# A graph-attention layer on one core: scatters of a second sort held between gathers, and record loads moved from the GpSimd queue to the Sync queue

## The chip, the cores and the metric

The kernel runs on one core of one Trainium2 chip. Its time is device time in microseconds (us). The kernel before took 1815.98 us, the median of three runs (1813.75 to 1820.42). One further execution was taken with the hardware profiler and gives all durations below; in it "start" counts from the beginning of the span. TensorE is called PE in the profile (its weight loads PEld), VectorE DVE, ScalarE ACT, GpSimd POOL, and SyncE SP, which only issues transfers here.

## The reference

A layer of masked attention with 4096 targets, 4096 sources, a width of 512 and 8 heads of 64, followed by a feed-forward network and a last normalisation. All arithmetic is float32. The adjacency matrix is sparse: some 17 sources to a target. Cut to what matters:

```python
hs = layer_norm(x, ln1_scale, ln1_bias)              # sources
ht = layer_norm(h_target, ln1_scale, ln1_bias)       # targets
q = (ht @ Wq + bq).reshape(T, 8, 64) / sqrt(64)
k = (hs @ Wk + bk).reshape(S, 8, 64)
v = (hs @ Wv + bv).reshape(S, 8, 64)
logits = where(adj != 0, einsum('thd,shd->hts', q, k), -1e30)
ctx = einsum('hts,shd->thd', softmax(logits), v).reshape(T, 512)
ht = layer_norm(ht + ctx @ Wo + bo, ln2_scale, ln2_bias)
out = ht + gelu(ht @ W1) @ W2
return layer_norm(x + out)                           # no scale, no bias
```

## The kernel before

**Sparse attention by gathers.** The kernel does not compute all 4096 x 4096 logits. It finds the neighbours of every target as a list of row numbers, writes keys and values of all sources into a DRAM table `kvd` (one row of 1024 floats per source), and fetches, for a tile of 128 targets, neighbour number j of each target with one indirect transfer. A tile needs as many gathers as its longest list. So that tiles are even, the targets are sorted by degree: `CAPS_A` and `CAPS_B` (L374) give how many neighbours the sorted tiles may have.

**Two parts.** The 32 row blocks are handled in two halves of 16, part 0 and part 1 (`PARTS`). For each half, `edges(i)` (L717) builds lists from the adjacency rows, and `sort(part)` (L808) computes where each target goes in the sorted order and scatters its *record* (degree, target number, two normalisation numbers and up to 24 neighbours: 29 words) into the DRAM table `recs_d[part]`. The scatter of part 0 runs before attention begins; the lists and the sort of part 1 run beside the attention over the first half (the stream `other_lists`, L1444), and its 16 scatters (L854, in the profile `rec<-R,kv`) stand on the GpSimd queue among the gathers.

**What the attention does per tile.** `prefetch(i)` (L971) loads the records of sorted tile i from `recs_d` into one of six `rec` buffers (L980, in the profile `rec<-rec`); `front(i)` gathers the targets' rows (`tq<-in_L_gnn_h_target_dram`), normalises and projects them. `issue(k)` (L1059) gathers the keys and values of group k, three neighbours at a time (L1076, issued through `gather`, L966, so that the profile shows L967, `kv<-kvd,rec`), into a ring of 17 slots, 20 from the second half on. VectorE multiplies keys with queries (L1220), sums them to logits (L1225), ScalarE takes exponentials (L1229, L1238), VectorE scales values (L1184), and TensorE adds them up by transposing them into one PSUM tile (L1192). When L1192 of a group has read its slots they are free for later gathers: group k waits for L1192 of group k-5 or k-6. `finish` (L1078) divides, applies Wo (L1116), takes the second normalisation (statistics on VectorE L697, the power -1/2 on GpSimd L687, its use L692 and L1134) and transposes (L1143) for the feed-forward network.

**Long lists.** Two tiles, sorted tile 15 (39 neighbours) and tile 17 (38), have more than the 24 neighbours that a record holds. For them `rest_of` (L769) gathers the rest (`gid<-rest_d,rec`), and VectorE picks the next neighbours in two rounds of L779 and L780, and counts them (L783, L786).

**Feed-forward.** `feed(g)` (L1310) runs per pair of tiles: W1 (L1325), GELU on ScalarE (L1328), W2 (L1334). `end` normalises and scatters the result rows (L1302, `out_dram<-xt,tags`; the rows of x come by `xt<-in_x_dram,tags`).

**What sets the order.** The streams attention, feed-forward, lists of the second half and weights are woven in program order by costs (`_weave`, L400). A scheduler then fixes each engine's queue ahead of the run: it may move an instruction ahead of, or behind, others on its engine where its own estimate of times says so, unless an edge forbids it. [...] `tc.issue_after(ins)` adds such an edge: what is written inside the block stays behind `ins` on that engine's queue, without a semaphore. On GpSimd the queue before has, after the first half's gathers have run for some time, 9 scatters in a row, three gathers, the power L687, 6 scatters, and a little later the last one. On the Sync queue all adjacency loads (L714) and all stores of list rests (L767) come before anything that the change puts there; after it stands only the read of the final flag (L1453).

Of the kernel before, what the change touches and what calls it, by code (L numbers as in the profile page):

```python
# [1 line left out]

# [15 lines left out]
P = 128  # L18
# [360 lines left out]
RW = E0 + RE  # L379
# [64 lines left out]
def adj_resnorm_kernel(  # L444
# [33 lines left out]
    nc = tc.nc  # L478
# [34 lines left out]
    recs_d = [dram.tile([n * P, RW], I32, name=f"rec{i}") for i, (_, n) in enumerate(PARTS)]  # L513
# [19 lines left out]
    with tc.tile_pool(name="keep", bufs=1) as keep:  # L533
# [17 lines left out]
        with ExitStack() as late:  # L551
# [22 lines left out]
            def turn_of(name, places):  # L574
                turns[name] += 1
                return places[turns[name] % len(places)]
# [132 lines left out]
            def quarter(i, h):  # L709
# [4 lines left out]
                nc.sync.dma_start(a, adj[i * P:(i + 1) * P, h * QW:(h + 1) * QW])  # L714
                return a

            def edges(i):  # L717

                part = 1 if i >= NA else 0
                rec = Rs[part][:, i - PARTS[part][0], :]  # L720
                cand = lp.tile([P, SEG, 8], U16, name="cand", bufs=2)
                for h in range(NQ):
                    n = i * NQ + h
                    while len(adjs) < min(n + 2, NT * NQ):
                        adjs.append(quarter(*divmod(len(adjs), NQ)))
                    a, adjs[n] = adjs[n], None

                    sg = turn_of("signs", signs)
                    nc.scalar.activation(sg, a, AF.Sign, accum_out=dpart[:, i, h:h + 1])  # L729
                    ahead = min(n + DEEP - 1, n + 3 + n // 2)  # L730
                    while len(adjs) < min(max(n + 3, min(ahead, RINGED * NQ)), NT * NQ):
                        adjs.append(quarter(*divmod(len(adjs), NQ)))
                    wd = sg.bitcast(U16)
                    nc.vector.tensor_tensor(wd, wd, lio, ALU.mult)
                    for s, (w0, w1) in enumerate(SEGS):
                        nc.vector.max(cand[:, h * SQ + s, :], wd[:, w0:w1])  # L736
                    if h == 1:
                        keep_rest()
                    if h % 2 and moms:
                        moments(moms.pop(0))  # L740
                    yield 2.0
                dec = dec_w
                nc.vector.tensor_single_scalar(dec[:, 0], cand, 255, op=ALU.bitwise_and)
                nc.vector.tensor_single_scalar(dec[:, 1], cand, 8, op=ALU.logical_shift_right)
                gid = lp.tile([P, 2 * SEG, 8], F32, name="gid")
                dec = dec.rearrange("p b s e -> p (b s) e")
                off = segoff.rearrange("p b q s -> p (b q s)")
                nc.vector.scalar_tensor_tensor(gid, dec, 0.0,
                                               off.unsqueeze(2).to_broadcast([P, 2 * SEG, 8]),
                                               op0=ALU.is_gt, op1=ALU.mult)  # L750
                nc.vector.tensor_add(gid, gid, dec)
                flat = gid.rearrange("p s e -> p (s e)")
                for r in range(RE // 8):
                    top = rec[:, E0 + r * 8:E0 + (r + 1) * 8]
                    nc.vector.max(top, flat)  # L755
                    if r + 1 < RE // 8:
                        nc.vector.match_replace(flat, top, flat, 0.0)
                held.append((rest_d[i * P:(i + 1) * P, :], flat))
                has = lp.tile([P, MAXE], F32, name="ehas")
                nc.vector.tensor_scalar(has[:, :RE], rec[:, E0:E0 + RE], 0.0, 0.0, op0=ALU.is_gt,  # L760
                                        op1=ALU.add, accum_out=cnt[:, i:i + 1])
                yield 4.0

            def keep_rest():

                while held:
                    nc.sync.dma_start(*held.pop())  # L767
# [40 lines left out]
            def sort(part):  # L808

                i0, n = PARTS[part]  # L810
                me = slice(i0, i0 + n)
                pool, R = lp, Rs[part]
                nc.vector.tensor_reduce(deg[:, me], dpart[:, me, :], AX.X, ALU.add)
                nc.vector.tensor_copy(R[:, :, DEG], deg[:, me])
                dif, rank = tools[:, 928:928 + n], tools[:, 944:944 + n]
                ranki, b16 = tools[:, 960:960 + n].bitcast(I32), tools[:, 976:984].bitcast(BF16)
                nc.vector.scalar_tensor_tensor(dif, deg[:, me], float(RE), cnt[:, me], op0=ALU.min,
                                               op1=ALU.not_equal)
                nc.vector.tensor_reduce(bad[:, 1 + part:2 + part], dif, AX.X, ALU.max)
                nc.vector.tensor_scalar(dif, deg[:, me], 0.0, float(NB - 1), op0=ALU.max,  # L820
                                        op1=ALU.min)
                nc.vector.tensor_scalar(b16, dif, -1.0, float(NB - 1), op0=ALU.mult, op1=ALU.add)
                if part:
                    oh = turn_of("wide", wide).bitcast(BF16)
                else:
                    oh = wp.tile([P, NB * n], BF16, name="oh")
                oh = oh[:, :NB * n].rearrange("p (b i) -> p b i", b=NB)
                nc.vector.tensor_tensor(oh, b16.unsqueeze(1).to_broadcast([P, NB, n]),
                                        bins.unsqueeze(2).to_broadcast([P, NB, n]), ALU.is_equal)
                ohf = oh.rearrange("p b i -> p (b i)")  # L830
                pos = turn_of("wide", wide).bitcast(F32)
                pos = pos[:, :NB * n].rearrange("p (b i) -> p b i", b=NB)
                posf = pos.rearrange("p b i -> p (b i)")
                w = NB * n // 2
                yield 6.0
                for c in range(2):
                    sl = slice(c * w, (c + 1) * w)
                    pt = ps.tile([P, w], F32, name="t", bufs=2)
                    nc.tensor.matmul(pt, ones_bf, ohf[:, sl], start=True, stop=True)
                    nc.vector.tensor_tensor_scan(posf[:, sl], one_c.to_broadcast([P, w]), pt,  # L840
                                                 0.0 if c == 0 else posf[:, c * w - 1:c * w],
                                                 op0=ALU.mult, op1=ALU.add)
                yield 4.0
                for c in range(2):
                    sl = slice(c * w, (c + 1) * w)
                    pa = ps.tile([P, w], F32, name="t" if part else "cps", bufs=2)
                    nc.tensor.matmul(pa, lower, ohf[:, sl], start=True, stop=True)
                    nc.vector.tensor_add(posf[:, sl], pa, posf[:, sl])
                nc.vector.tensor_mul(pos, pos, oh)
                nc.vector.tensor_reduce(rank, pos.rearrange("p b i -> p i b"), AX.X, ALU.add)  # L850
                nc.vector.tensor_copy(ranki, rank)
                yield 10.0
                for i in range(n):
                    ins = nc.gpsimd.indirect_dma_start(  # L854
                        out=recs_d[part][:, :],
                        out_offset=bass.IndirectOffsetOnAxis(ap=ranki[:, i:i + 1], axis=0),
                        in_=R[:, i, :], in_offset=None)

                    tc.declare_no_dep(ins.ins, group=f"scatter{part}", reason="other rows")
                    tc.add_to_no_dep_group(f"scatter{part}", ins.ins)  # L860
                    yield 3.0 if part else 1.3
                done.add(part)
# [98 lines left out]
                        yield cost  # L961


            recs, tqs, h2Ts, done, ready, latest, newest = {}, {}, {}, set(), [], [], []

            def gather(dst, table, idx):  # L966
                nc.gpsimd.indirect_dma_start(  # L967
                    out=dst, out_offset=None, in_=table[:, :],
                    in_offset=bass.IndirectOffsetOnAxis(ap=idx, axis=0))

            def prefetch(i):  # L971
                if i >= NT or i in recs:
                    return
                r0 = TILES[i][0]
                part = 1 if r0 >= PARTS[1][0] * P else 0
                assert part in done
                r0 -= PARTS[part][0] * P
                rec = sp.tile([P, E0 + MAXE], I32, name="rec", bufs=6)

                nc.gpsimd.dma_start(rec[:, :RW], recs_d[part][r0:r0 + P, :])  # L980
                recs[i] = rec

            def front(i, idle=0):
# [503 lines left out]
```

## Time and profile before

| | |
|---|---|
| median of three runs | 1815.98 us (1813.75 to 1820.42) |
| the profiled execution | 1817.49 us |
| its span, first to last instruction | 1815.5 us |
| mean TensorE clock granted, share of full speed | 0.967 |
| TensorE busy | 1677.8 us, 92% |
| VectorE busy | 1436.5 us, 79% |
| ScalarE busy | 1224.1 us, 67% |
| GpSimd busy | 982.2 us, 54% |
| HBM traffic | 430.75 MB read, 30.89 MB written, 254 GB/s over the span |

The span starts with projections and lists of the first half; attention proper begins at about 300 us, the scatters of the second sort run from 627 to 665 us, the last gather starts at about 1663 us, and the rest is feed-forward work. "Busy" counts the time in which an instruction executes. [...] An engine idle in front of an instruction is shown with the instruction that released it ("<-"); "<-issue" means that the profile shows nothing it waited for. A busy share is an average over stages, so the question is always which wait ends last in the stage at hand.

### The profile page before, as it was taken

What the parts mean: (1) busy time and instruction counts of PE and PEld (TensorE: products, weight loads), DVE (VectorE), ACT (ScalarE), POOL (GpSimd) and SP (SyncE); (2) the same over time, 40 slices, a digit from 0 to 9 for tenths busy, and PEclk for the clock granted to TensorE, in tenths of its full rate; (3) what the DMA queues carried; (4) which work ended last, traced back from release to release, by engine and by line L of the source; (5) the groups of instructions that cost most, each with busy time, mean ns of one, the idle gap of its engine ahead of it and who ended that gap; (6) DMA issues with size and microseconds to landing.
All of it is one profiled execution on the core that took longest, in us unless ns stands there. A gap on an engine that the chain in (4) does not pass through costs nothing. (4 is left out here: it accounts for less than half of the span.)

```text
span 1815.5 us, 22973 instructions
## 1 busy us (share of the span) xinstructions
PE 1677.8 (92%) x7030; PEld 1097.9 (60%) x7030; DVE 1436.5 (79%) x2660; ACT 1224.1 (67%) x3121; POOL 982.2 (54%) x834
## 2 busy tenths in 40 slices
PE   7989984597999979999999989999999999999997
PEld 3434442465766656766776757666666666666664
DVE  6989876899999837777978989978878797988200
ACT  5767654487987736766778868877777676787311
POOL 1000144656566676766678788867575665763101
PEclk9999996698999989999999999999999999999998
DMA  9999968989887557777878878787776776774000
GB/s 344 366 380 372 344 198 319 404 287 332 271 305 256 201 173 243 258 255 267 273 263 302 293 260 295 249 285 250 241 266 222 248 251 238 244 248 153 18 6 26
DMA packets 140269, 463.26 MB, mean 255 GB/s; under 512 B 16500, under 2 KB 21672, under 8 KB 140136
## 3 DMA queue, kind: packets, MB, share of 16 engines
q0 software_dynamic: 96656, 342.64, 55.8%
q1 hardware_dynamic: 35664, 95.98, 15.0%
q10 hardware_dynamic: 7816, 23.08, 3.3%
q8 instruction: 58, 0.95, 0.2%
q14 instruction: 75, 0.61, 0.1%
HBM read 430.75 MB, written 30.89 MB: 254 GB/s over the span
## 5 line engine op out<-in xcount | busy, mean ns | idle before, releaser
L967 POOL DMA_INDIRECT kv<-kvd,rec x603 | 758.1, 1257 | 347.5 <-PE cps L1192 139.7
L1334 PE MATMUL po<-w,gt 128*128 128x512 f32 x1024 | 466.4, 598 | 16.2 <-ACT gt L1328 16.2
L1325 PE MATMUL pf<-h2T,w 128*128 128x256 f32 (+1 forms) x2176 | 465.9, 368 | 0.1
L1325 PEld LDWEIGHTS pf<-h2T,w 128*128 128x128 f32 x2176 | 389.3, 191 | 64.5 <-issue 20.3
L1220 DVE TENSOR_TENSOR kv<-kv,tq 128x1536 f32<-128x1536 f32 (+2 forms) x211 | 351.6, 1675 | 68.3 <-DMA kv<-kvd,rec 56.2
L1204 ACT ACTIVATE kv<-kv,pa 128x64 f32<-128x64 f32 x1520 | 391.0, 336 | 4.3
L1225 DVE TENSOR_REDUCE lg<-kv 128x24 f32<-128x1536 f32 (+2 forms) x211 | 350.1, 1666 | 1.4
L1334 PEld LDWEIGHTS po<-w,gt 128*128 128x128 f32 x1024 | 188.8, 192 | 212.4 <-issue 194.3
L1192 PEld LDWEIGHTS cps<-ident,kv 128*128 128x128 f32 x2008 | 240.2, 145 | 109.4 <-issue 59.2
L1192 PE MATMUL cps<-ident,kv 128*128 128x128 f32 x2008 | 264.5, 280 | 44.1 <-DVE kv L1184 24.5
L1184 DVE TENSOR_TENSOR kv<-kv,p 128x1024 f32<-128x1024 f32 (+1 forms) x211 | 251.0, 1193 | 22.8 <-ACT p L1229 20.3
L687 POOL TENSOR_TENSOR n_rs<-n_ve,mhalf 128x2 f32<-128x2 f32 (+2 forms) x51 | 50.8, 997 | 329.1 <-DVE n_ve L680 165.3
L729 ACT ACTIVATE kv<-kv 128x1024 uint8<-128x1024 int32 x128 | 134.9, 1056 | 100.0 <-DMA kv<-in_adj_dram 51.7
L1328 ACT ACTIVATE gt<-pf 128x512 f32<-128x512 f32 x128 | 76.4, 597 | 93.8 <-PE pf L1325 75.8
L1328 ACT ACT_TABLE_LOAD x104 | 133.4, 1283 | 1.7
L736 DVE MAX8 cand<-kv 128x8 uint16<-128x103 uint16 (+1 forms) x640 | 131.8, 252 | 0.8 <-DVE R L755 0.2
L930 PE MATMUL pq<-wk,h2T 128*128 128x512 f32 x256 | 120.8, 616 | 12.1 <-ACT tq L932 7.2
L1012 PE MATMUL t<-wq,tq 128*128 128x512 f32 x256 | 118.2, 605 | 5.6 <-ACT tq L1006 5.6
L930 PE MATMUL pq<-wv,h2T 128*128 128x512 f32 x256 | 115.5, 594 | 6.4 <-ACT kv L729 3.0
L1229 ACT ACTIVATE p<-lg 128x24 f32<-128x24 f32 (+2 forms) x179 | 39.2, 219 | 113.0 <-DVE lg L1225 88.8
L1116 PE MATMUL t<-wo,rb 128*128 128x512 f32 x256 | 115.2, 592 | 0.0
L930 PEld LDWEIGHTS pq<-wk,h2T 128*128 128x128 f32 x256 | 48.9, 197 | 69.9 <-issue 55.2
(160 smaller groups left out, 1582.2 us busy)
## 6 DMA issues: line engine op xcount, KB each, us to landing
kv<-in_adj_dram SPq DMA_DIRECT2D x128, 512.0 KB
kvd<-tq ACTq DMA_DIRECT2D x24, 512.0 KB
kv<-kvd,rec POOLq DMA_INDIRECT x603
kv<-in_L_gnn_h_target_dram SPq DMA_DIRECT2D x32, 256.0 KB
kv<-in_x_dram SPq DMA_DIRECT2D x15, 512.0 KB
rest_d<-gid SPq DMA_DIRECT2D x32, 160.0 KB
w<-in_L_gnn_W_dram SPq DMA_DIRECT2D x4, 1024.0 KB
kvd<-kv ACTq DMA_DIRECT2D x8, 512.0 KB
```

Source lines behind the costliest of these rows:

```text
L729: nc.scalar.activation(sg, a, AF.Sign, accum_out=dpart[:, i, h:h + 1])
L736: nc.vector.max(cand[:, h * SQ + s, :], wd[:, w0:w1])
L930: nc.tensor.matmul(pkv, hT[:, kc, j * P:(j + 1) * P], w[:, kc, :], start=kc == 0, stop=kc == KC - 1)
L967: nc.gpsimd.indirect_dma_start(out=dst, out_offset=None, in_=table[:, :], in_offset=bass.IndirectOffsetOnAxis(ap=idx, axis=0))
L1184: nc.vector.tensor_tensor(v4, v4, p[:, j0:j0 + m, :].unsqueeze(3) .to_broadcast([P, m, H, HD]), ALU.mult)
L1192: nc.tensor.matmul(cps[:, c, :], kv[:, j, D + c * P:D + (c + 1) * P], ident, is_transpose=True, start=j0 + j == 0 and c == 0, stop=j0 + n ...
L1204: newest[:] = [nc.scalar.mul(v, v, pa[:, hd:hd + 1]).ins]
L1220: nc.vector.tensor_tensor(kv[:, :n, :D], kv[:, :n, :D], tq[:, :D].unsqueeze(1).to_broadcast([P, n, D]), ALU.mult)
L1225: nc.vector.tensor_reduce(lg[:, :n, :], kv[:, :n, :D].rearrange("p j (h d) -> p j h d", h=H), AX.X, ALU.add)
L1325: nc.tensor.matmul(pf[:, k, :], w1[(f0 + k) // KC][:, kc, (f0 + k) % KC * P:((f0 + k) % KC + 1) * P], h2T[:, kc, :w], start=kc == 0, stop= ...
L1328: nc.scalar.activation(gt, pf, AF.Gelu_apprx_tanh)
L1334: nc.tensor.matmul(po[j], gt[:, k, j * P:(j + 1) * P], w2[(f0 + k) // KC][:, (f0 + k) % KC, :], start=False, stop=f0 + k == FC - 1, skip_g ...
```

## The change

Three edits. First, `gather` remembers the instruction that it issued, in the list `issues`. Second, each scatter of `sort` is written inside `behind(issues)`, which is `tc.issue_after` of the newest gather if there is one, and nothing otherwise; so part 0's scatters, before any gather, are as they were, and each scatter of part 1 stays behind the gather written last before it. Third, the record loads of part 1 (16 of 32) are issued from SP instead of GpSimd.

```diff
+            def behind(ins):
+                return tc.issue_after(ins[-1]) if ins else nullcontext()
...
                 for i in range(n):
-                    ins = nc.gpsimd.indirect_dma_start(
-                        out=recs_d[part][:, :],
-                        out_offset=bass.IndirectOffsetOnAxis(ap=ranki[:, i:i + 1], axis=0),
-                        in_=R[:, i, :], in_offset=None)
+                    with behind(issues):
+                        ins = nc.gpsimd.indirect_dma_start(
+                            out=recs_d[part][:, :],
+                            out_offset=bass.IndirectOffsetOnAxis(ap=ranki[:, i:i + 1], axis=0),
+                            in_=R[:, i, :], in_offset=None)
...
-            recs, tqs, h2Ts, done, ready, latest, newest = {}, {}, {}, set(), [], [], []
+            recs, tqs, h2Ts, done, ready, latest, newest, issues = {}, {}, {}, set(), [], [], [], []
 
             def gather(dst, table, idx):
-                nc.gpsimd.indirect_dma_start(
+                issues[:] = [nc.gpsimd.indirect_dma_start(
                     out=dst, out_offset=None, in_=table[:, :],
-                    in_offset=bass.IndirectOffsetOnAxis(ap=idx, axis=0))
+                    in_offset=bass.IndirectOffsetOnAxis(ap=idx, axis=0)).ins]
...
-                nc.gpsimd.dma_start(rec[:, :RW], recs_d[part][r0:r0 + P, :])
+                (nc.sync if part else nc.gpsimd).dma_start(rec[:, :RW], recs_d[part][r0:r0 + P, :])
```

The scheduler rearranges what is free to move. TensorE's queue comes out the same, instruction for instruction. On GpSimd, where the first scatter stood, the queue is now: 1 scatter, the record load of tile 14, 3 gathers, 2 scatters, the power L687, an output scatter, 3 gathers, 2 scatters, the row gathers and the second output scatter, and then groups of one to three gathers with one or two scatters after each; the last two scatters stand behind the gid gather of tile 15. On SP the 16 record loads follow each other behind the last store of list rests. ScalarE's queue has two more loads of its activation table and some neighbouring instructions exchanged; on VectorE some neighbours are exchanged, and the second round of L779 and L780 for tile 15 stands further back.

More of the change, by code (lines that the diff above doesn't have):

```diff
@@ L1 @@
-from contextlib import ExitStack
+from contextlib import ExitStack, nullcontext
 import concourse.bass as bass
```

## The prediction

> **What bounds the kernel now.** I read the page first, then the busy time by stretch of time, then what TensorE waited for, then the timelines of TensorE, VectorE and GpSimd around the scatters that the change moves. Page, part 1 (busy us, share of the span, instructions):
>
> ```profile
> PE 1677.8 (92%) x7030; PEld 1097.9 (60%) x7030; DVE 1436.5 (79%) x2660; ACT 1224.1 (67%) x3121; POOL 982.2 (54%) x834
> ```
>
> TensorE is idle for 1815.5 - 1677.8 = 138 us in all. Its instruction list is identical in both kernels, so the change can only alter how long it waits or at which clock it runs. In the groups of GpSimd instructions (count, busy us, mean ns, then idle time before them), the kinds at issue are these:
>
> ```profile
> L967 POOL DMA_INDIRECT kv<-kvd,rec x603 | 758.1, 1257 | 347.5 <-PE cps L1192 139.7 <-issue 121.0 <-DVE kv L1188 32.8
> L854 POOL DMA_INDIRECT rec<-R,kv x32 | 34.6, 1083 | 46.3 <-DVE cand L736 35.7 <-issue 8.7 <-DVE kv L851 1.5
> L980 POOL DMA_DIRECT2D rec<-rec x32 | 18.9, 593 | 22.3 <-DVE p L1083 8.9 <-DVE n_ve L680 5.3 <-DMA rec<-R,kv 4.9
> ```
>
> With the 0.30 us that stands before each in the timeline, a gather costs GpSimd 1.56 us, a scatter 1.38, a record load 0.9. The busy time by stretch (PE, PEld, DVE, ACT, POOL busy with counts, then TensorE clock, DMA share, GB/s) puts the loss in one place:
>
> ```profile
> 640.00:680.00 40.00, 30.05 (x132) 20.25 (x131) 15.70 (x13) 16.23 (x41) 30.97 (x28) 0.87 0.56 187
> 680.00:720.00 40.00, 38.33 (x178) 26.48 (x176) 30.56 (x40) 23.94 (x68) 23.80 (x22) 1.00 0.78 268
> 720.00:760.00 40.00, 40.00 (x179) 26.93 (x180) 31.61 (x37) 29.78 (x82) 28.80 (x23) 1.00 0.68 218
> ```
>
> The timelines of TensorE, ScalarE and VectorE there (start, us, instruction, in brackets the idle time before it and its releaser):
>
> ```profile
> 671.55 5.51 PE L1334 MATMUL po<-w,gt 128*128 128x512 f32 x8 [9.95 <-ACT gt L1328]
> ...
> 718.29 1.53 PE L1192 MATMUL cps<-ident,kv 128*128 128x128 f32 x12 [1.50 <-DVE kv L1184]
> ...
> 667.93 0.22 ACT L1229 ACTIVATE p<-lg 128x24 f32<-128x24 f32 x1 [12.92 <-DVE lg L1225]
> ...
> 664.35 1.76 DVE L1220 TENSOR_TENSOR kv<-kv,tq 128x1536 f32<-128x1536 f32 x1 [9.37 <-DMA kv<-kvd,rec]
> ```
>
> And GpSimd:
>
> ```profile
> 623.75 1.77 POOL L967 DMA_INDIRECT kv<-kvd,rec  x1 [0.30 <-issue]
> 627.06 1.01 POOL L854 DMA_INDIRECT rec<-R,kv  x1 [1.53 <-DVE kv L851]
> ...
> 640.16 0.97 POOL L967 DMA_INDIRECT kv<-kvd,rec  x1 [0.30 <-issue]
> ...
> 656.12 0.98 POOL L967 DMA_INDIRECT kv<-kvd,rec  x1 [0.30 <-PE cps L1192]
> ...
> 668.26 1.98 POOL L967 DMA_INDIRECT kv<-kvd,rec  x1 [0.30 <-issue]
> ...
> 695.50 0.58 POOL L980 DMA_DIRECT2D rec<-rec  x1 [4.50 <-DVE p L1083]
> ...
> 701.42 0.96 POOL L967 DMA_INDIRECT gid<-rest_d,rec  x1 [0.30 <-issue]
> 702.40 0.73 POOL L687 TENSOR_TENSOR n_rs<-n_ve,mhalf 128x2 f32<-128x2 f32 x1
> ```
>
> The reader is to see a chain: 9 + 6 + 1 scatters stand between gather triples, so the triples leave at 640, 656 and 668 instead of every few us. VectorE waits for the second, ScalarE's exponential for VectorE, the GELU behind it in ScalarE's queue comes late, and TensorE loses 9.95 us. Its next eight matmuls take 5.51 us against 3.60 elsewhere, 1.9 us more. Together with the 1.50 us at 718 this place costs 13.4 us.
>
> [...]after 1.50 us there is no such loss (1.53 us for twelve). [...]
>
> **The change part by part.** *Scatters.* The edge holds each scatter behind the gather written before it. [...] Up to the gid gather there are the same 24 ring gathers as before and 14 scatters instead of 16. So GpSimd has only 2 x 1.38 = 2.8 us less to do, and I walk the list:
> - first scatter ends 628.1; the record load needs the buffer that VectorE's L1083 of tile 8 frees at 630.9, so it starts at 631.2 (3.1 us idle that the before did not have, as there the load came later) and ends 631.8; triple to 636.5; 2 scatters to 639.3; power to 640.0 (before 644.4);
> - output scatter, waiting for ScalarE's L1298, 641.3 to 642.4; triple to 647.1 (before 659.6). Triples land 4.65 us after their last issue (643.65 to 648.30; 659.62 to 664.35), so VectorE has it at 651.7, not 664.35;
> - 2 scatters 649.9; tq, xt and output to 654.3; the second xt gather waits for that output to land, 3.5 us as at 663.5 to 666.94 before, and ends 659.1;
> - triple 663.8 (before 672.7); scatter 665.2; triple 669.9 (676.5); 2 scatters 672.7; triple 677.4; scatter 678.8; single 680.4; 2 scatters 683.1; triple 687.8; 2 scatters 690.6; triple 695.3; scatter 696.6; two gathers 699.7; tq 701.2; record 702.1; power 702.8; gid starts 703.1 (before 701.42).
>
> TensorE with this supply: the GELU wanted at 661.5 is there at 651.7 + 1.75 + 1.75 + 3.6 = 658.9, so the 9.95 us and the slow clock go, and TensorE runs 11.9 us ahead. Then it spends the lead: about 2.6 us before L1012 (needs L1006, behind the exponential of a single gather that lands at 685), 1.6 us at L1143 (needs the power at 702.8), and at 709 it reaches the L1192 that stood at 718.29. That one is tied to the gid gather: VectorE's queue has the two list steps L779 and L780 ahead of the next tile's L1220. Gid at 703.1 lands 3.5 us later (4.0 and 3.1 before), 706.6; 1.07 + 0.68 + 0.57 us of VectorE, since part of the list work moved further back; L1220 at 708.9 against 708.68; L1192 at 718.5. A stall of 9 us there brings the clock loss of 1.9 us. Sum: stalls 2.6 + 1.6 + 9.1 + 1.9 = 15.2 against 13.4, thus +1.8 us. This uses mean durations; the timeline's commonest are 0.94 and 0.97 us, and with 1.25 and 1.27 us a step the gid gather comes some 6 us sooner, giving -5. Bounds -6 and +6; I take 0, between them. The move fails to gain because GpSimd's ring waits (139.7 us of "PE cps") were partly filled by the bunched scatters, and the interleaved order leaves idle 3.1 us at the record and 3.2 at the xt gather, then is busy without a gap.
>
> *Records through SP.* 16 loads leave GpSimd, 16 x 0.9 = 14 us plus waits (2.25 us at 1013, 3.5 us at 793). Where GpSimd waits for ring slots this is worth nothing: 720 to 840, where TensorE is full. From 900 to 1200 GpSimd is busy 241 of 300 us and the gaps fill most of the rest; there TensorE loses 3.58 us at 989, 5.00 at 1089 (VectorE waiting for a power queued behind gathers) and 3.40 at 1204 with 1.6 of slow clock. Loads in front of these: one, one, three, of 0.9 us each, counted since the last ring wait; I take -3.5 us, bounds 0 and -9. On SP nothing is queued behind the loads but the final flag, since all adjacency and rest stores stand ahead of them; their wait for the 16 scatters ends about 721 (703.1, the gid gather, six more gathers, two scatters and the landing), and the first record was loaded at 749 before. Cost 0; if late, it delays the tq gather of tile 16.
>
> *Order of other engines.* ScalarE gets 2 more table loads (1.28 us each) and VectorE some swaps: bounds -1 and +3, I take +0.5, as ScalarE has slack.
>
> Sum on the profiled span: 0 - 3.5 + 0.5 = -3. Its execution took 1817.49 us (span 1815.5 and 2.0 around it), the median of the runs is 1815.98; the same -3 there gives 1813.
>
> **Rivals.** (a) The lead is kept: GpSimd runs at its commonest durations, and the list chain is not binding, so -10 in the window and -3 later: 1803. For it: triples land 12 us sooner. Against: L1192 at 718 already waited for VectorE before, no slack. (b) Slower, the gid gather: the same chain, but GpSimd later than my walk, because each further ring wait or long gather (up to 4.2 us in the trace) shifts gid, and each us behind 703 is one us for TensorE. At 713 it is +10, with a second clock loss of 1.9 at L1143 and nothing won later, +12.5: 1828. It decides from gid later than about 709. (c) The change doesn't do what it says: excluded, the order of instructions shows scatters spread and 16 loads on SP.
>
> **How the numbers follow.** About no change 0.53 (own range 1807 to 1825), (a) 0.17, (b) 0.30. A measurement tells 0.5%, about 9 us, from no change. With both tails, 1803 to 1829.
>
> **What would show it.** Right: no TensorE wait at 661, a wait of 5 to 10 us about 709 to 718 in front of L1192, gid near 703, fewer stalls between 980 and 1210. Wrong: TensorE unbroken through 720 (rival a), or gid after 709 (rival b), or a tq gather waiting for a record from SP.

## The result, and the profile after

The changed kernel takes 1824.03 us, the median of ten runs (1822.12 to 1831.26), against 1818.63 us for ten runs of the kernel before on the same chip (1813.75 to 1823.52). The ratio is 1.0033, with a 95% interval of 1.0019 to 1.0047: slower by 5 to 6 us, where -3 was forecast. The profiled execution has a span of 1829.5 us, 14.0 more than the one of before. It is at the upper end of the runs, so the first question is how much of these 14 us the change made.

What TensorE waited for between 627 and 745 us, in the kernel before (what waits, for what: us in total, times, longest):

```profile
PE po L1334 <- ACT gt L1328: 9.9, 1, 9.9
PE cps L1192 <- DVE kv L1184: 1.5, 1, 1.5
```

The same view of the kernel after, where all lines below L858 have moved down by 4 (L1192 is now L1196):

```profile
PE cps L1196 <- DVE kv L1188: 5.8, 1, 5.8
PE t L1016 <- ACT tq L1010: 3.9, 1, 3.9
PE t L1147 <- DVE tq L1021: 1.9, 1, 1.9
```

The large stall is gone, and the three waits that the prediction listed stand in its place. The busy time by stretch of the kernel after (columns as in the prediction) shows it too:

```profile
640.00:680.00 40.00, 40.00 (x193) 28.54 (x193) 21.93 (x19) 19.77 (x53) 29.74 (x26) 1.00 0.59 189
680.00:720.00 40.00, 31.14 (x123) 19.58 (x121) 19.28 (x27) 15.87 (x39) 29.75 (x27) 0.91 0.65 210
720.00:760.00 40.00, 37.25 (x163) 26.09 (x164) 30.31 (x40) 32.70 (x87) 26.39 (x21) 0.91 0.72 236
```

TensorE is full up to 680 us and pays afterwards: 108.4 us busy in 120, and 108.4 us before (30.05 + 38.33 + 40.00). Equal busy time is not equal work: the same matmuls can be busy for longer, and the clock granted between 680 and 760 us is 0.91, against 1.00 before. Two of the waits of the kernel after, and then two places of the kernel before (the same eight matmuls as L1016, and a wait further on):

```profile
694.00 6.58 PE L1016 MATMUL t<-wq,tq 128*128 128x512 f32 x8 [3.94 <-ACT tq L1010]
722.75 2.82 PE L1196 MATMUL cps<-ident,kv 128*128 128x128 f32 x12 [5.81 <-DVE kv L1188]
```

```profile
698.92 3.60 PE L1012 MATMUL t<-wq,tq 128*128 128x512 f32 x8
819.16 5.10 PE L1334 MATMUL po<-w,gt 128*128 128x512 f32 x8 [2.90 <-ACT gt L1328]
```

GpSimd and VectorE at the place where the lead is lost (timelines; in brackets the idle time before the instruction and its releaser):

```profile
703.59 0.62 POOL L984 DMA_DIRECT2D rec<-rec  x1
704.21 0.76 POOL L687 TENSOR_TENSOR n_rs<-n_ve,mhalf 128x2 f32<-128x2 f32 x1
708.10 1.05 POOL L971 DMA_INDIRECT gid<-rest_d,rec  x1 [3.13 <-DMA rec<-rec]
```

```profile
711.11 0.09 DVE L782 MATCH_VALUE_LOAD gid<-rec,gid 128x8 int32 x1 [5.94 <-DMA gid<-rest_d,rec]
...
713.15 3.42 DVE L1224 TENSOR_TENSOR kv<-kv,tq 128x1536 f32<-128x1536 f32 x2
```

VectorE stands idle for 5.94 us until the gid gather of the long tile has landed, and the product of the next tile (L1224) is queued behind it. TensorE's L1196 at 722.75 waits for that.

To see where the time goes, compare the start of the same instruction in both traces along the run. The execution after is 3.0 us late from about 450 us on, before the first instruction that differs; a second execution of the same kernel (after_again, below) is 1.9 us early there, so this is chance. TensorE is then 9.0 us early at 683 us, 6.2 late at 745, 2.4 late at 840 and 3.2 late at 1262 us. So the stretch that the change rearranges costs 3.2 us up to 745 us, which come back by 840 us. At the last output scatter the execution is 5.2 us late, and at the end of the span 14.0. The jump is behind the last piece of work. In the kernel before and then after:

```profile
1806.68 1.04 POOL L1302 DMA_INDIRECT out_dram<-xt,tags  x1 [1.38 <-DVE flag L1372]
```

```profile
1811.84 1.04 POOL L1306 DMA_INDIRECT out_dram<-xt,tags  x1 [1.38 <-DVE flag L1376]
```

From there to the end of the span it is 1815.5 - 1806.7 = 8.8 us before, and 1829.5 - 1811.8 = 17.7 us after. The waits of SP's queue in this tail, before and then after:

```profile
SPq L1482 <- PEq L1482: 2.0, 2, 1.4
```

```profile
SPq L1486 <- PEq L1486: 9.3, 2, 8.8
```

Line 1482 (1486 after) is the end of the program, where all engines meet. The view names TensorE's sequencer as the releaser, which is inferred from semaphores. The question is who was still at work. The instructions of that line in the kernel before and then after (engine, operation, count: shortest/median/longest ns, first and last start):

```profile
L1482 POOLq DRAIN  x3: 44/107/1952, 1812.7 to 1815.2; - x3
...
L1482 PEldq DRAIN  x2: 8/8/8, 1811.7 to 1815.0; - x2
```

```profile
L1486 POOLq DRAIN  x3: 44/107/9302, 1819.4 to 1829.3; - x3
...
L1486 PEldq DRAIN  x2: 8/8/8, 1816.7 to 1829.0; - x2
```

TensorE is at the meeting point at 1816.7. GpSimd begins its DRAIN at 1819.4 and needs 9302 ns for it, against 1952 ns before. The step ahead of it on GpSimd, before and then after:

```profile
L1454 POOLq INC_SWDGE_SEM  x1: 660/660/660, 1812.0 to 1812.0; - x1
```

```profile
L1458 POOLq INC_SWDGE_SEM  x1: 2455/2455/2455, 1816.9 to 1816.9; - x1
```

Together they are 11.76 us instead of 2.61, that is 9.15 more, which is the 8.9 us of the tail but for 0.2. The trace gives the durations and cannot show by itself that they hold no wait; that they are equal to a few ns in kernels whose order differs speaks for it (9302 and 9297 ns for the DRAIN in after, sp_only, act_recs and spare1 of the experiments below, 2455 ns for INC_SWDGE_SEM in after, act_recs and spare1).

The 14.0 us are then 3.0 of chance, 2.2 up to the last scatter (nearly all of it between 1262 and 1280 us, where the eight L1016 took 5.40 us instead of 3.70), and 8.9 of tail.

### The profile page after: what moved, and what is told of

It is laid out like the page before. It is cut to its first block, busy times and chain, and to the rows that moved or that the text cites. A ratio compares the mean times of both kernels' runs of the same rounds, so it can differ in the third digit from the quotient of the medians.

```text
span 1829.5 us, 23066 instructions
## 1 busy us (share of the span) xinstructions
PE 1683.7 (92%) x7030; PEld 1102.0 (60%) x7030; DVE 1436.1 (78%) x2660; ACT 1227.0 (67%) x3123; POOL 973.5 (53%) x818
## 3 DMA queue, kind: packets, MB, share of 16 engines
q1 hardware_dynamic: 37968, 96.22, 15.2%
## 5 line engine op out<-in xcount | busy, mean ns | idle before, releaser
L1338 PE MATMUL po<-w,gt 128*128 128x512 f32 x1024 | 463.9, 595 | 4.7 <-ACT gt L1332 4.5
L1224 DVE TENSOR_TENSOR kv<-kv,tq 128x1536 f32<-128x1536 f32 (+2 forms) x211 | 351.7, 1675 | 64.1 <-DMA kv<-kvd,rec 52.7
L1196 PE MATMUL cps<-ident,kv 128*128 128x128 f32 x2008 | 267.6, 282 | 49.1 <-DVE kv L1188 36.8
L1196 PEld LDWEIGHTS cps<-ident,kv 128*128 128x128 f32 x2008 | 242.9, 146 | 115.2 <-issue 51.5
L1338 PEld LDWEIGHTS po<-w,gt 128*128 128x128 f32 x1024 | 187.8, 191 | 199.6 <-issue 193.3
L687 POOL TENSOR_TENSOR n_rs<-n_ve,mhalf 128x2 f32<-128x2 f32 (+2 forms) x51 | 51.1, 1001 | 336.9 <-DVE n_ve L680 150.6
L1016 PE MATMUL t<-wq,tq 128*128 128x512 f32 x256 | 121.9, 621 | 9.3 <-ACT tq L1010 9.3
```

The costliest lines, as they stand in the source:

```text
L1196: nc.tensor.matmul(cps[:, c, :], kv[:, j, D + c * P:D + (c + 1) * P], ident, is_transpose=True, start=j0 + j == 0 and c == 0, stop=j0 + n ...
L1224: nc.vector.tensor_tensor(kv[:, :n, :D], kv[:, :n, :D], tq[:, :D].unsqueeze(1).to_broadcast([P, n, D]), ALU.mult)
L1338: nc.tensor.matmul(po[j], gt[:, k, j * P:(j + 1) * P], w2[(f0 + k) // KC][:, (f0 + k) % KC, :], start=False, stop=f0 + k == FC - 1, skip_g ...
```

## The experiments

Sixteen kernels ran. Those of a section share one chip and its runs of the kernel before, but for gid_nopin, which ran on its own; so ratios are comparable throughout, and times only within a section. "sp" in a name is a kernel with free scatters, "gid" one whose extra gather is held. The edits are shown against the changed kernel, or against the kernel named in brackets, and dots stand between two places of a kernel. The numbers of the tail are in the table at the end.

### Which part of the change makes the loss

Theory: the pinned scatters lose more in the stretch around 700 us than they gain. Rival: the record loads on SP's queue make the loss. Four kernels. The first is the change once more, the second has all records on GpSimd's queue with the scatters pinned, the third has the scatters free and the records of the second half on SP:

```diff
 pin_only
-                (nc.sync if part else nc.gpsimd).dma_start(rec[:, :RW], recs_d[part][r0:r0 + P, :])
+                nc.gpsimd.dma_start(rec[:, :RW], recs_d[part][r0:r0 + P, :])
 sp_only
-                    with behind(issues):
-                        ins = nc.gpsimd.indirect_dma_start(...)
+                    ins = nc.gpsimd.indirect_dma_start(...)
```

The fourth is the change with the extra gather of the two long tiles held behind the gather written before it, so that the scheduler cannot pull it forward:

```diff
 gid_late
-                gather(flat, rest_d, rec[:, TGT:TGT + 1])
+                with behind(issues):
+                    gather(flat, rest_d, rec[:, TGT:TGT + 1])
```

> The changed kernel once more, to see which of its differences repeat. If the waits of TensorE in front of L1016 (3.94 us), L1147 (1.86) and L1196 (5.81, about 720 us) come from the order of the GpSimd queue, they come again within 0.5 us. The 3.0 us by which the first profile was later already at 465 us, before any changed instruction, is chance if it comes again with another size (0 to 3), and belongs to the program if it is 3.0 again. Ratio to before 1.002 to 1.005.

> Only the scatters are pinned; all records are loaded by GpSimd. Theory (the loss is made by the pinned scatters in front of the gid gather): waits of about 4, 2 and 6 us before L1016, L1147 and L1196 as in the changed kernel, no wait of 10 us in front of L1338, ratio 1.002 to 1.005. Rival (the loads through SP make the loss): ratio 0.999 to 1.001.

> Only the records of the second part go through SP; scatters in bunches of 9, 6 and 1 as before. Theory: the 9.95 us wait in front of L1334 stays, the waits of 5.0 us at 1089 and 3.4 at 1204 stay too, ratio 0.998 to 1.000. Rival (SP makes the loss): ratio 1.002 to 1.005 and new waits after 840 us. The forecast on record had the loads worth 3.5 us, ratio 0.998.

> The changed kernel with the gid gathers held behind the newest gather as well, so that VectorE's list steps for tile 15 no longer stand in front of tile 10's products. Theory (the gid gather, late on GpSimd and first on VectorE, makes the wait at L1196): the 5.81 us wait about 720 us goes with its slow clock, 4 to 7 us less than the changed kernel, ratio to before 0.999 to 1.001; the waits before L1016 and L1147 stay. Rival (the gathers themselves come too late, whatever stands ahead on VectorE): the wait stays at 4 us or more, ratio 1.002 to 1.005. A wait may come up instead where tile 15 begins, about 900 us, if its lists come too late there.

| kernel | us, median | ratio to before, 95% interval |
|---|---|---|
| after_again | 1825.24 | 1.0032 (1.0018 to 1.0046) |
| pin_only | 1816.70 | 1.0004 (0.9993 to 1.0015) |
| sp_only | 1821.31 | 1.0030 (1.0019 to 1.0042) |
| gid_late | 1818.78 | 1.0014 (1.0000 to 1.0028) |

The first theory falls: pinning alone is within the measurement of no change. sp_only has the whole loss. Two expectations were missed on the way. In after_again the three waits are 3.47, 3.62 and 3.21 us, so their sum comes near the first (10.3 against 11.6) and their single sizes, expected within 0.5 us, do not. And in gid_late the wait in front of L1197 (L1196 of the change) did not go: it is 4.19 us, though the matmuls behind it start at 712.8 instead of 722.8 us (1.8 of that by chance); the wait of L1147 is the one that went.

The trace of sp_only has less waiting than before, not more. What TensorE waited for between 640 and 840 us in the kernel before:

```profile
PE po L1334 <- ACT gt L1328: 12.8, 2, 9.9
PE cps L1192 <- DVE kv L1184: 1.5, 1, 1.5
PE t L1099 <- ACT h2T L1147: 0.6, 2, 0.4
```

And in sp_only:

```profile
PE po L1334 <- ACT gt L1328: 10.3, 2, 9.0
PE cps L1192 <- DVE kv L1184: 0.2, 1, 0.2
PE t L1099 <- ACT h2T L1147: 0.2, 1, 0.2
```

Its last output scatter starts at 1797.8 us, 8.9 us earlier than before (3.9 of them by chance: it has this lead at 620 us already), and its span ends at 1815.7, 0.2 us later. All four kernels show the same split: without records on SP 8.5 us from the last scatter to the end, with them 17.4 to 18.2.

### Is it SP's queue, or what GpSimd no longer does

New theory A: GpSimd's two last steps hang on what its own queue has started over the run. It started 765 transfers in before and pin_only, and 749 in the others. Rival B: SP's queue, having carried the records, costs the time.

```diff
 act_recs (scatters free)
-                (nc.sync if part else nc.gpsimd).dma_start(rec[:, :RW], recs_d[part][r0:r0 + P, :])
+                (nc.scalar if part else nc.gpsimd).dma_start(rec[:, :RW], recs_d[part][r0:r0 + P, :])
 sp_spare (sp_only, and beside each record load of the second half)
+                    nc.gpsimd.dma_start(spare_d[:, :], recs_d[0][:P, :])
...
 gid_spare (gid_late, and before attention)
+            spare = wp.tile([16, RW], F32, name="spare")
+            for j in range(16):
+                nc.gpsimd.dma_start(spare[j:j + 1, :], x[j:j + 1, :RW])
 gid_pool (gid_late)
-                (nc.sync if part else nc.gpsimd).dma_start(rec[:, :RW], recs_d[part][r0:r0 + P, :])
+                nc.gpsimd.dma_start(rec[:, :RW], recs_d[part][r0:r0 + P, :])
```

> The kernel before with the 16 record loads of the second part on ScalarE's DMA queue, scatters where they were. In the four kernels with the records on SP, GpSimd's last two steps (INC_SWDGE_SEM, then DRAIN, at the program's end) take 2.46 and 9.30 us, in before and pin_only 0.66 and 1.95; that is 9.1 us of the 9 that their ends last longer. Theory A, it hangs on how many transfers GpSimd's own queue has started (765 in before and pin_only, 749 in the others): also 749 here, so 2.46 and 9.30 us, and 17 to 18.5 us from the last scatter's start to the end of the span. Theory B, it hangs on SP's queue having carried the records: 0.66 and 1.95 us, and 8.4 to 9 us. Up to the last scatter both expect 1796 to 1808 us.

> sp_only with a spare copy of the same shape (a record block of the first part into an unused DRAM tensor) issued by GpSimd at each of the 16 record loads, so that GpSimd starts 765 transfers again, while the records still come through SP. Theory A (number of GpSimd's transfers): 0.66 and 1.95 us for its last two steps, 8.4 to 9 us from the last scatter to the end, and sp_only's 1821.3 less 9.1: 1812, ratio 0.998 (0.996 to 1.000). Theory B (SP's queue): 2.46 and 9.30 us stay, 1821, ratio 1.003.

> gid_late (the change, and the wide tiles' extra gather held behind the gather before it) with 16 small loads of 116 B by GpSimd in the first 20 us, which nobody reads: 765 transfers[...]. Theory A: gid_late's 1818.8 less 9.1: 1809.7, ratio 0.9965 (0.995 to 0.998). [...] Theory B: 1819, ratio 1.0015.

> gid_late with the records of both parts on GpSimd's queue as before: pinned scatters and the held extra gather alone. Theories A and B: 8.4 to 9 us at the end. In gid_late's trace the stretch from 640 to 835 us is 9 us shorter than in before, in pin_only's equal, in sp_only's 5 us shorter. If the held gather makes that gain by itself, 1811, ratio 0.9975; if it needs the records off GpSimd's queue, 1815 to 1817, ratio 1.000.

act_recs has nothing of the records on SP, and its end is that of the changed kernel:

```profile
L1482 POOLq DRAIN  x3: 44/107/9302, 1804.9 to 1814.8; - x3
```

sp_spare and then gid_spare have the records on SP and a short DRAIN, shorter than in the kernel before:

```profile
L1485 POOLq DRAIN  x3: 44/107/894, 1835.2 to 1836.7; - x3
```

```profile
L1490 POOLq DRAIN  x3: 50/109/885, 1806.6 to 1808.1; - x3
```

B is out: what matters is that the loads left GpSimd, wherever they went. A holds in its direction, but 765 transfers gave 1952 ns in one mixture and 894 and 885 in two others, so it is not the number alone. Nor is it the number of packets that the profile counts for GpSimd's queue: it is 96656 in all three mixtures.

By time: gid_spare 1809.60 us, ratio 0.9951 (0.9935 to 0.9967); gid_pool 1816.34, 0.9997 (0.9986 to 1.0009); act_recs, one run, 1816.81 against a median of 1818.2 for before. The held gather alone gains nothing, then; it needs the records off GpSimd's queue. sp_spare took 1836.63 us, ratio 1.0093 (1.0079 to 1.0107), some 25 us over the 1812 expected, and that is a mistake of the experiment. The copies had no reader, so the scheduler was free to put nine of them close together near 300 us, and they waited for each other there:

```profile
POOL spare L983 <- DMA spare<-rec: 28.6, 9, 5.7
```

TensorE is 0.7 us early at 280 us and 23.1 late at 450. So the time of sp_spare says nothing of the question; the length of its DRAIN does.

### A gradual account or a step

> gid_spare with one small load in place of 16. What SP's queue carries is the same in both, so theory B is out after act_recs (9.30 us without SP) and sp_spare (0.89 us with SP). What is left: GpSimd's last DRAIN takes 9.30 us with 749 transfers of one kind, 1.95 with these and 16 record loads, 0.89 with these and 16 spare ones. Theory C, a gradual account [...]: (9.30 - 0.89)/16 = 0.53 us per load, so 8.8 us here. Theory D, a step [...]: either 9.3 and above, or already some 1 to 2 us.

> gid_spare with eight small loads: theory C, halfway: DRAIN 5.1 us and INC_SWDGE_SEM 1.4. Theory D: 9.3 or more, or at most 2, nothing near 5. Up to the last scatter as gid_spare, 1798 to 1806 us.

> gid_spare with 24 small loads: theory C: even lower than 0.89 us[...]. Theory D: risen a little from 0.89, by as much per load as the time rises between the steps. Up to the last scatter as gid_spare.

> gid_late with every second record load of the second part on SP and the others on GpSimd. Half of the 16 moved loads are GpSimd's again. Theory C: DRAIN (9.30 + 1.95)/2 = 5.6 us, and the time between gid_late's 1818.8 and gid_pool's 1816.3, less what half the lead is worth: 1814 to 1818, ratio 0.999. Theory D: 1.95 us or a little less or more, or 9.30; with about 2 us the time is 1810 to 1814, ratio 0.997.

The first three are gid_spare with 1, 8 and 24 small loads in place of 16. gid_half is gid_late with `nc.sync if part and i % 2 else nc.gpsimd` for the records. With one small load and then with eight:

```profile
L1490 POOLq DRAIN  x3: 50/109/9297, 1805.0 to 1814.8; - x3
```

```profile
L1490 POOLq DRAIN  x3: 50/109/803, 1801.5 to 1802.9; - x3
```

A step, somewhere between 750 and 757 transfers of this mixture, and no halfway value: theory C, a gradual account (5.1 us with eight), falls, and theory D, a step, holds. Behind the step the time rises slowly with what is added. gid_half took 1812.64 us, ratio 0.9960 (0.9940 to 0.9980), in the range that D gave. The others ran once: 1816.91, 1804.93 and 1808.24 us, with the kernel before at a median of 1817.53.

### The tail alone taken out, and what is left of the change

If the tail is the whole loss, giving back just enough transfers should remove it. The three kernels have the records of the last eight tiles on GpSimd's queue again, far behind the stretch at 700 us: the change itself (after_last8), sp_only (sp_last8) and gid_late (gid_last8). gid_nopin is gid_last8 with the scatters free.

```diff
-                (nc.sync if part else nc.gpsimd).dma_start(rec[:, :RW], recs_d[part][r0:r0 + P, :])
+                (nc.sync if part and i < 24 else nc.gpsimd).dma_start(rec[:, :RW], recs_d[part][r0:r0 + P, :])
```

> The changed kernel with the records of its last eight tiles on GpSimd's queue again (757 transfers); the stretch around 640 to 840 us has its records on SP as in the change. If GpSimd's end is the whole loss: DRAIN 1.3 us as in gid_half, 9 us or less from the last scatter to the end of the span plus at most 1, and after_again's 1825.2 less 8.5: 1816 to 1817, ratio 0.9995 (0.998 to 1.001). If the loss has another source as well (the pinned scatters' waits at 690 to 725 us), ratio 1.002 or more with the short end.

> sp_only with the records of its last eight tiles on GpSimd's queue: without the long end, records through SP alone should give the gain that the prediction put at 3.5 us (0 to 9): 1812 to 1814, ratio 0.998 (0.996 to 0.999). If that gain is not there, 1.000.

> gid_late with the records of its last eight tiles on GpSimd's queue: the order of gid_spare in the stretch 640 to 840 us, the short end, and no idle loads: 1808 to 1812, ratio 0.9955 (0.994 to 0.998). If the eight loads cost the later tiles as much as they save at the end, 1815 or more.

> gid_last8 with the scatters of the second part left free, as in before; the extra gather stays behind the gather before it. sp_last8 is this kernel with the extra gather free (0.9981), after_last8 the one with the scatters pinned and the gather free (0.9996), gid_last8 the one with both held (0.9955). If the held gather makes the gain by itself, 0.994 to 0.996 here too. If the pinned scatters and the held gather belong together (with the scatters free, the 10 us stall near 665 us stays, and a late gather can't take it away), 0.998 (0.9965 to 0.9995), 1811 to 1814 us.

| kernel | scatters | extra gather | us, median | ratio to before, 95% interval |
|---|---|---|---|---|
| after_last8 | pinned | free | 1814.95 | 0.9996 (0.9983 to 1.0008) |
| sp_last8 | free | free | 1811.04 | 0.9981 (0.9969 to 0.9993) |
| gid_last8 | pinned | held | 1808.74 | 0.9955 (0.9938 to 0.9973) |
| gid_nopin | free | held | 1816.30 | 0.9992 (0.9981 to 1.0003) |

The changed kernel with the short tail is level with the kernel before. Its ratio went from 1.0032 to 0.9996, so 0.36% of 1815, about 6.5 us, against 8.2 us by which the tails of the profiled runs differ (17.7 and 9.5); both intervals together leave room for that. The two other pairs agree: from sp_only to sp_last8 0.49%, 8.9 us, with tails that differ by 8.0, and from gid_late to gid_last8 0.59%, 10.7 us, with 7.7. gid_nopin shows whether the held gather does without the pinned scatters: with the scatters free, the stall of before is still there,

```profile
PE po L1338 <- ACT gt L1332: 9.7, 1, 9.7
```

and holding the extra gather does not help. gid_last8 is faster than both kernels of the case, by 0.45% against before, and has no loads that nobody reads. In its trace the same view (627 to 745 us) has

```profile
PE cps L1197 <- DVE kv L1189: 3.4, 1, 3.4
PE t L1017 <- ACT tq L1011: 1.4, 1, 1.4
```

and the two extra gathers stand 200 us later than in the change, where they start at 708 and 796 us:

```profile
L972 POOL DMA_INDIRECT gid<-rest_d,rec x2: 951/1164/1378, 915.0 to 1013.5; - x2
```

The tails, by profiled run: the transfers that GpSimd issued, its two last steps, the start of the last output scatter, and the time from there to the end of the span, in us.

| kernel | transfers | INC_SWDGE_SEM | DRAIN | last scatter | tail |
|---|---|---|---|---|---|
| before | 765 | 0.66 | 1.95 | 1806.7 | 8.8 |
| pin_only | 765 | 0.66 | 1.95 | 1801.2 | 8.5 |
| gid_pool | 765 | 0.66 | 1.95 | 1802.1 | 8.7 |
| after | 749 | 2.46 | 9.30 | 1811.8 | 17.7 |
| after_again | 749 | 2.46 | 9.30 | 1807.8 | 18.2 |
| sp_only | 749 | 2.46 | 9.30 | 1797.8 | 17.9 |
| gid_late | 749 | 2.46 | 9.30 | 1798.7 | 17.4 |
| act_recs | 749 | 2.46 | 9.30 | 1797.3 | 17.8 |
| spare1 | 749 + 1 small | 2.46 | 9.30 | 1797.3 | 17.8 |
| spare8 | 749 + 8 small | 0.38 | 0.80 | 1796.0 | 7.1 |
| gid_spare | 749 + 16 small | 0.40 | 0.89 | 1801.0 | 7.4 |
| spare24 | 749 + 24 small | 0.52 | 1.38 | 1798.7 | 7.7 |
| sp_spare | 749 + 16 copies | 0.39 | 0.89 | 1829.6 | 7.4 |
| gid_half | 749 + 8 records | 0.50 | 1.30 | 1804.0 | 9.7 |
| after_last8 | 749 + 8 records | 0.50 | 1.30 | 1801.2 | 9.5 |
| sp_last8 | 749 + 8 records | 0.50 | 1.30 | 1797.8 | 9.8 |
| gid_last8 | 749 + 8 records | 0.50 | 1.30 | 1798.1 | 9.7 |
| gid_nopin | 749 + 8 records | 0.50 | 1.30 | 1803.7 | 9.0 |

In the five last rows GpSimd's DRAIN ends 2.0 to 2.8 us before the end of the span, and 0.8 us in all others: SP's own last steps come late there. Why stays open.

## Why the prediction was wrong, point by point

- *The old stalls go, 13.4 us.* Right. No wait at 661, and TensorE full to 680 us. At 683 us it is 9.0 us ahead, 12.0 without the 3.0 of chance; the walk had 11.9.
- *New stalls of 2.6 before L1012, 1.6 at L1143, 9.1 at L1192, and 1.9 of slow clock, 15.2 in all.* The places were right, two sizes were not. The waits measured 3.94, 1.86 and 5.81, together 11.6 for 13.3 predicted. The slow clock cost 5.3 us for 1.9 predicted: the eight L1016 took 6.58 us instead of 3.60, and the twelve L1196, the four L1103 and the eight L1338 behind the third wait took 2.27 us more than elsewhere. The sum is 11.6 + 2.98 + 2.27 = 16.9, and against the 13.4 of before that is +3.4 (3.2 by the starts), where the walk had +1.8 and the prediction took 0. The prediction put no slow clock behind its first wait, of 2.6 us. That was the author's estimate, and near this size the traces show both: 2.90 us of waiting at 819 us in the kernel before were followed by eight matmuls in 5.10 us, and 2.74 us at 1280 us in the kernel after by eight in 5.40, against 3.60 elsewhere; after 2.29 us at 1276 us in the kernel before they took 3.70, and after the 1.50 us at 718 us twelve L1192 took 1.53 us, against 1.47 elsewhere. In the other two traces with this order the stretch costs 3.9 (after_again) and 1.2 us (after_last8). That the pinned scatters bring nothing by themselves was right (pin_only: +0.7 us of 1816, from -1.3 to +2.7).
- *The gid gather binds L1192, at 703.1.* It started at 708.10, of which 3.0 us belong to this execution as a whole. The rest is a wait that the walk did not have, though it had the order: only the power stands between the gather and the load of the record that holds its indices, and the gather waited 3.13 us for that load to land. The trace of before has the like at 793 us, the 3.5 us that the prediction names. The role was right: with the gather held back by 200 us, and the scatters pinned, the kernel gains 0.41% (0.9996 to 0.9955).
- *Records through SP, -3.5, bounds 0 and -9.* The size came out, the reason given for it is not shown. sp_last8, which has little else, gains 0.19%, 3.4 us (1.3 to 5.6). But the stalls that it was to shorten are nearly as they were: the waits of 5.00 and 3.40 us at 1089 and 1204 us are 5.01 and 3.41 in the kernel after, and the one of 3.58 at 989 us fell to 2.37, but to 2.54 in pin_only too, where no record went to SP. In sp_only TensorE's waits fell from 14.9 to 10.7 us between 640 and 840 us, in part where the prediction wrote "worth nothing" (720 to 840). Of these 4.2 us, 2.0 lie behind 800 us, and there pin_only has them too: of all eighteen traces only that of before has more than 1.4 us of waiting there, so it may be chance. Where the 3.4 us are won stays open. The gain also does not add to the pinning: with both and the short tail, -0.7 us is left (from -3.1 to +1.5).
- *"On SP nothing is queued behind the loads but the final flag ... Cost 0."* This is the step that failed. It looked at the queue that receives the loads, and there it is right: SP waits 368.6 us for the flag, and no tq gather waits for a record. The prediction did not ask what the queue that loses them does at the end. The term that was taken as nothing is +9.15 us in the trace. With it the prediction's own sum would have been -3 + 9.15 = +6 us, against +5.4 between the medians. That it comes so near is in part luck, since the stretch up to 745 us cost 3.2 us where the sum has 0, and the time between 745 and 840 us, of which the sum says nothing, gave 3.8 back. The page of before gave no way to compute it, since its 1.95 us for the DRAIN does not say what it depends on; but the tail of 8.8 us was there to be seen, and the sum assumed without a word that it stays.
- *Rival (b), slower through a late gid gather.* The side was right and the cause was not: the gather came about where that rival begins to count (708.1, and 709 there), and after_last8, which has waits of 5.6 and 4.2 us at two of the same places, is not slower. Rival (a), a lead that is kept, did not happen: TensorE was 9 us ahead of the kernel before at 683 us and 6 us behind it at 739, 3 of them chance.
- *ScalarE's order, +0.5.* Too small to be seen in any of these runs.

## What to carry to other kernels

When transfers leave a queue, compare the end of the run too: the time from the last piece of work to the end of the span, and who is last at the meeting point, in a trace of either kernel. A span that grew need not mean that the work ended later. And a bundle of edits is best tried in all its halves: here, with the short tail, pinning alone lost 0.04%, moving records alone gained 0.19%, each of the three pairs of these two and the held gather gained 0.03% to 0.08%, and all three together 0.45%. Of these only the 0.19% and the 0.45% are clear of no change.

## What was not expected of the hardware

GpSimd's last two steps, INC_SWDGE_SEM and DRAIN, went with the transfers that its queue had started over the run, by a step: together 11.76 us with 749 or 750 (after, spare1), 1.18 us with seven small loads more (spare8). On one side of the step all kernels agree to 5 ns in DRAIN (9297 and 9302 ns), whatever their order. On the other it rose with what was added, by 0.082 us for each of eight more record loads (1.30 to 1.95 us), and less evenly for the small ones (0.80, 0.89 and 1.38 us with 8, 16 and 24). All these kernels change the count of GpSimd's instructions together with its transfers, and none adds an instruction that is not a transfer, so the two are told apart only in so far as 765 transfers, with equally many instructions, gave two lengths (1.95 and 0.89 us). No run here shows what the two steps do in that time, at which count between 750 and 757 the step lies, or whether another kernel has it, and this stays open.
